# Mamba steps of 16 channels by 8 states: new step layout, a text position for every piece, and a reordered last layer

## The chip, the cores and the metric

The kernel runs on one core of one Trainium2 chip. The metric is the device time of one execution in microseconds (us); the number of record is the median over the runs of the kernel before. Engine names are those of the profile: PE (TensorE matmul), PEld (its weight loads), DVE (VectorE), ACT (ScalarE), POOL (GpSimd), SP (SyncE, which here issues DMAs).

## The reference

Four layers follow one another on an image of 2 x 64 x 96 x 96, all in float32. Cut to what matters:

```python
# layer 0: attention over all 9216 pixels of an image, then a 1x1 convolution with batch norm
x = bn(conv1x1(softmax(theta(x) @ phi(x)) @ g(x))) + x
# layer 1: depthwise and 1x1 convolution, batch norm, relu; layer norm; one Mamba over L = 9216
# layer 2: for the rows, then for the columns of the image: RMS norm, a forward and a backward
#          Mamba over L = 96, joined by a linear map, plus the input
# layer 3: a 3x3 filter per group of channels, its taps = tanh(W mean(x)), plus x

def mamba(h):                       # 128 inner channels d, 16 states s
    xm, z = split(h @ in_proj.T)
    xc = silu(causal_conv4(xm) + convd_b)
    dt, B, C = split(xc @ x_proj.T)             # 4, 16, 16 columns
    dt = softplus(dt @ dt_proj.T + dt_proj_b)
    A = -exp(A_log)                             # [d, s]
    # for each t:
    hc = hc * exp(dt[..., None] * A) + dt[..., None] * B[:, None, :] * xc[..., None]
    y  = einsum('bds,bs->bd', hc, C)
    return ((y + xc * Dp) * silu(z)) @ out_proj.T
```

## The kernel before

**Layer 0** (`layer0_direct`) is not touched. It fills the first 2400 us of the profiled execution.

**Layers 1 and 2** are a stream of 120 *units*, run by the class `Mamba`. A unit is one Mamba over a chunk of `CH` = 768 positions for one image of the batch: 24 units of layer 1, which carry their state from chunk to chunk (`u.carry`), and 96 units of layer 2, each with 8 whole sequences of 96 ("fresh"; the odd ones run backward). The 2048 recurrences of a unit (128 channels by 16 states) are laid on 128 partitions in 16 *steps*. A chunk has two halves of `HALF` = 384 positions; a half has 16 *turns* and a step takes two of them at once, 128 x 768 elements. In a turn, partition 8 s + i holds state s and channel 8 n + i (mod 128 over the turns), so 8 channels meet all 16 states and every turn rotates which channel a partition sees.

A step runs through these pieces:
- `read` (SP, L912): two DMAs bring dt and u = dt * xc, spread over the partitions, from a DRAM copy (`rows`, written twice one below the other by `step_write`, so that a turn is a plain window of 128 rows) into one of 6 `spread` buffers
- `decay` (ACT, L919): two Exp with a scale per partition, into an `h` buffer (9 of them)
- `inputs` (DVE, L929): u times B, into one of two PSUM places; B is spread to all partitions by the matmul of `shared` (L923), once for each half
- `scan` (DVE, L944, or L940 twice for a carried state): hc = decay * hc + input; then POOL multiplies by C (L945)
- `gather` (PE, L954): two matmuls of 128 x 128 sum over the states and put the channels in place in `y`; the first of a half adds xc * Dp (L951)

Around the steps stand the pieces of a unit: norm, convolution (L821/L827, read at L832), gate, silu (between two loads of ACT's table, L841 and L842), softplus (`step_read`, `step_exp`, `step_log` on ACT, then `step_kept`, `step_sum`, `step_dt` on POOL: L872, L875, L878), `step_u` (L882), `step_write`, C (`c_mm`, L898), and at the end `y_half` (L958), `y_read` (L961), `y_gate` (POOL, L964) and the `tail` projection (L987/L990). All but the steps' own share one PSUM tile of two banks (tag `m`).

**Order.** Tiles and semaphores are the framework's, but `run` issues everything in an order written out by hand, and each engine executes its instructions in the order of that text. `PIECES` gives each piece an offset in whole steps against its unit, alike for both layers; within a step the order is fixed (reads, decays, inputs, scan, gathers, pieces that read PSUM, the others). The first unit's head runs ahead alone, and one unit's worth of empty steps follows it. At two steps of every unit `next(other)` advances a generator that finishes the image of layer 1 and prepares the weights of the four Mambas of layer 2 (`mamba_weights`, L629 to L667, and `joined`) in the free space of `xa`.

**Layer 3** copies the image with mirrored borders into `upper` (DVE, L1250) and `lower`, computes the taps (L1255 to L1277), and filters: PE in four sets of rows with tiles of 32 x 32 (L1294, 16 matmuls for each tap, copied out by ACT at L1303) and DVE for the 28 rows at the top (L1313). It stands in a section of its own behind the Mamba stage.

Of the kernel before, what the change touches and what calls it, by code (L numbers as in the profile page):

```python
# [25 lines left out]
P = 128  # L26
# [9 lines left out]
NMAMBA = 5  # L36

# [34 lines left out]
def setup(ctx, tc, x, cols, mats, dtw):  # L72
# [42 lines left out]
    k.minus = const.tile([P, 1], FP, name="minus")  # L115
    nc.vector.memset(k.minus, -1.0)
# [91 lines left out]
def layer0_direct(k, scale, bias, pre):  # L208
# [9 lines left out]
    with (  # L218
# [19 lines left out]
        def product(lhsT, rhs, m, n):  # L238
            p = bank("m")[:m, :n]
            nc.tensor.matmul(p, lhsT=lhsT, rhs=rhs, start=True, stop=True)  # L240
            return p
# [321 lines left out]

class Carver:
# [16 lines left out]
def mamba_tables(k, pool):  # L581

    nc = k.nc
    G = P // 8
    t = SimpleNamespace()

    t.member = pool.tile([P, 8], FP, name="member")
    nc.vector.reduce_sum(t.member, k.ident.rearrange("p (g i) -> p i g", i=8), axis=AX.X)  # L590
    t.group = pool.tile([P, 2, G], FP, name="group")
    for j in range(2):
        nc.vector.reduce_sum(t.group[:, j], k.ident.rearrange("p (g i) -> p g i", i=8), axis=AX.X)

    pair = pool.tile([P, 2, P], FP, name="pair")
    nc.vector.tensor_copy(pair, k.ident.unsqueeze(1).to_broadcast([P, 2, P]))
    pair = pair.rearrange("p j c -> p (j c)")
    t.gather = [pair[:, P - 8 * n : 2 * P - 8 * n] for n in range(G)]

    t.centre = pool.tile([P, 2, C], FP, name="centre")  # L600
    for j in range(2):
        nc.vector.tensor_add(t.centre[:, j], k.ident[:, :C], k.ident[:, C:])
        nc.vector.tensor_scalar_add(t.centre[:, j], t.centre[:, j], -1.0 / C)
    t.centre = t.centre.rearrange("p j c -> p (j c)")
    return t


def scratch(k, t, pool):


    G = P // 8
    t.turned = pool.tile([P, G, G], FP, name="turned")
    two = t.group.rearrange("p j g -> p (j g)")
    for n in range(G):
        k.nc.vector.tensor_copy(t.turned[:, n], two[:, G - n : 2 * G - n])
    t.placed = pool.tile([P, D_STATE, 8], FP, name="placed")
    t.rates = pool.tile([P, P // 8, P // 8], FP, name="turned_rates")


def mamba_weights(k, w, pool, product, tables, i):  # L620
# [4 lines left out]
    G = P // 8  # L625


# [3 lines left out]
    nc.vector.tensor_mul(  # L631
        tables.placed,
        tables.member.unsqueeze(1).to_broadcast([P, D_STATE, 8]),
        a.unsqueeze(2).to_broadcast([P, D_STATE, 8]),
    )
    p = product(tables.placed.rearrange("p s i -> p (s i)"), tables.group[:, 0], P, G)
    yield
    nc.vector.tensor_mul(tables.rates, tables.turned, p.unsqueeze(1).to_broadcast([P, G, G]))
    w.rates = pool.tile([P, G], FP, name=f"rates{i}")
    nc.vector.reduce_sum(w.rates, tables.rates, axis=AX.X)  # L640
# [23 lines left out]
    bc = pool.tile([P, 2, D_STATE, 8], FP, name=f"bc{i}")  # L664
    for j in range(2):
        at = DT_RANK + j * D_STATE
        nc.vector.tensor_copy(bc[:, j], x_w[:, at : at + D_STATE].unsqueeze(2).to_broadcast([P, D_STATE, 8]))  # L667
    w.gate_w = in_w[:, P:]
    w.bc = [bc[:, j].rearrange("p s i -> p (s i)") for j in range(2)]
# [5 lines left out]
class Mamba:  # L675
# [15 lines left out]
    STEPS = P // 8  # L691
    READ = 5
    DECAY = 3
# [15 lines left out]
    def product(self, lhsT, rhs, m, n):  # L709
        p = self.ps_m.tile([P, 2 * NB], FP, tag="m", name="mm")[:m, :n]  # L710
        self.nc.tensor.matmul(p, lhsT=lhsT, rhs=rhs, start=True, stop=True)
        return p
# [44 lines left out]
    def norm_square(self, u):  # L757

        if u.carry:
            u.norm.x = self.work("xn", D_CONV - 1 + CH)  # L760
            u.sq = self.work("sq", bufs=1)
# [15 lines left out]
    def image_1(self, u):  # L777
        self.image_copy(u, 1)
        if u.norm.unit is u and not u.carry:
            u.sq = self.work("sq", bufs=1)  # L780
# [69 lines left out]
    def step_read(self, u):  # L850
# [5 lines left out]
        u.kept = self.by_half(self.work("kept", bufs=1))  # L856
# [4 lines left out]
    def step_exp(self, u):  # L861
        nc = self.nc
        nc.scalar.activation(u.e, u.e, AF.Exp, scale=-1.0)
        nc.scalar.activation(u.kept, u.e, AF.Identity, bias=1.0)
        nc.scalar.activation(u.kept, u.kept, AF.Identity, bias=self.k.minus)  # L865
# [5 lines left out]
    def step_kept(self, u):  # L871
        self.nc.gpsimd.tensor_sub(u.kept, u.e, u.kept)  # L872

    def step_sum(self, u):
        self.nc.gpsimd.tensor_add(u.log, u.log, u.kept)  # L875

    def step_dt(self, u):
        self.nc.gpsimd.tensor_add(u.dt, u.dt, u.log)  # L878
# [9 lines left out]
    def step_write(self, u):  # L888
        u.rows = self.dram.tile([2 * P, 2 * CH], FP, tag="rows", name="rows")
        for j in range(2):  # L890
            self.nc.sync.dma_start(out=u.rows[j * P : (j + 1) * P], in_=u.both)

    def c_mm(self, u):
        u.p = self.mm([(u.w.bc[1], self.halves(u.xc))])

    def c_read(self, u):
        u.C = self.work("C")
        self.nc.scalar.copy(u.C, u.p)  # L898
# [4 lines left out]
    def turns(step):  # L903
        half, m = divmod(step, Mamba.STEPS // 2)
        return half, (2 * m, 2 * m + 1)

    def read(self, u, step):
        half, turns = self.turns(step)
        u.dtu[step] = self.work("spread", 2 * CH, bufs=6)
        for q, n in enumerate(turns):  # L910
            row = u.rows[8 * n : 8 * n + P, bass.ts(half, CH)]
            self.nc.sync.dma_start(out=u.dtu[step][:, bass.ts(q, CH)], in_=row)  # L912

    def decay(self, u, step):

        h = u.h[step] = self.work("h", bufs=9)
        for q, n in enumerate(self.turns(step)[1]):
            dt = u.dtu[step][:, q * CH : q * CH + HALF]
            self.nc.scalar.activation(h[:, bass.ts(q, HALF)], dt, AF.Exp, scale=u.w.rates[:, n : n + 1])  # L919

    def shared(self, u, half):

        self.nc.tensor.matmul(self.B, lhsT=u.w.bc[0], rhs=u.xc[:, bass.ts(half, HALF)], start=True, stop=True)  # L923

    def inputs(self, u, step):

        bx = self.places[step % 2][1].rearrange("p (q t) -> p q t", q=2)
        x = u.dtu[step].rearrange("p (q a t) -> p q a t", q=2, a=2)[:, :, 1]
        self.nc.vector.tensor_mul(bx, x, self.B.unsqueeze(1).to_broadcast([P, 2, HALF]))  # L929

    def scan(self, u, step):
        nc = self.nc
        half, turns = self.turns(step)
        h, bx = u.h[step], self.places[step % 2][1]
        h2 = h.rearrange("p (q t) -> p q t", q=2)
        if u.carry:
            state = u.carry[:, turns[0] : turns[1] + 1]
            for q in range(2):
                at = bass.ts(q, HALF)
                nc.vector.tensor_tensor_scan(h[:, at], h[:, at], bx[:, at], state[:, q : q + 1], ALU.mult, ALU.add)  # L940
            nc.gpsimd.tensor_copy(state.unsqueeze(2), h2[:, :, HALF - 1 :])
        else:
            way = slice(None, None, -1) if u.rev else slice(None)
            nc.vector.tensor_tensor_scan(h[:, way], h[:, way], bx[:, way], 0.0, ALU.mult, ALU.add)  # L944
        nc.gpsimd.tensor_mul(h2, h2, u.C[:, bass.ts(half, HALF)].unsqueeze(1).to_broadcast([P, 2, HALF]))  # L945

    def gather(self, u, step):

        half, turns = self.turns(step)
        if turns[0] == 0:  # L950
            self.nc.tensor.matmul(self.y, lhsT=u.w.direct, rhs=u.xc[:, bass.ts(half, HALF)], start=True, stop=False)  # L951
        for q, n in enumerate(turns):
            rhs, stop = u.h[step][:, bass.ts(q, HALF)], n == self.STEPS - 1
# [467 lines left out]
```

## Time and profile before

| | us |
|---|---|
| runs shown | 7492.55, 7496.15, 7505.91; median 7496.15 |
| profiled execution, own time | 7498.15 |
| its span, first to last instruction | 7496.4 |
| first product of a Mamba step starts (L929) | 2449.9 |
| last scan ends | 7428.8 |
| last set of PE in layer 3 ends | 7491.5 |

The mean granted TensorE clock is 0.972 of full speed. Times of single instructions come from the profiled execution. A line of a group reads: source line, engine, operation, output and inputs with shapes, count, then busy time and mean duration, then the engine's idle time just before those instructions and what ended most of it. Since consecutive instructions of an engine overlap a little in the records, the pitch between two starts is shorter than a mean duration.

### The profile page before, as it was taken

To read this page: it belongs to the slowest core of one execution; us is meant where nothing else is said; L and a number is where in the kernel's file an instruction comes from. 1 tells how busy PE (TensorE), PEld (TensorE's weight loads), DVE (VectorE), ACT (ScalarE), POOL (GpSimd) and SP (SyncE) were. 2 spreads that over 40 slices of the span, in tenths; PEclk is the share of its full clock that TensorE was granted. 3 is DMA by queue.
4 is the path that set the end of the run, shared out by engine and by line. 5 is a ranking of instruction groups with operands and counts; after the bars stand their busy time and mean duration, and the time that the engine had idled before them with its cause. 6 is when DMAs were issued, how large, how long until landed. Compare 5 with 4: busy or idle time off the path is not lost.

```text
span 7496.4 us, 106738 instructions
## 1 busy us (share of the span) xinstructions
PE 6776.0 (90%) x35828; PEld 3025.7 (40%) x35828; DVE 6881.7 (92%) x5965; ACT 5307.7 (71%) x7425; POOL 4857.1 (65%) x3219
## 2 busy tenths in 40 slices
PE   9999999999998888888888888888898888888887
PEld 3333333333332344443444444444444444444443
DVE  6778787888886799999999999999999999999998
ACT  5555555555555777777877788888788787787884
POOL 0000000000000799998989999999999999999995
PEclk9999999999998899999999999999999999999998
DMA  1000000000000799998999999999999999999996
GB/s 46 1 1 1 1 1 1 3 5 6 6 6 29 279 322 326 327 326 302 352 330 342 345 354 351 351 350 349 355 350 353 353 351 354 352 351 350 354 353 227
DMA packets 595263, 1727.63 MB, mean 230 GB/s; under 512 B 66312, under 2 KB 68620, under 8 KB 594320
## 3 DMA queue, kind: packets, MB, share of 16 engines
q1 hardware_dynamic: 594264, 1719.41, 63.1%
q8 instruction: 283, 4.64, 0.2%
q14 instruction: 276, 2.26, 0.1%
q10 hardware_dynamic: 440, 1.32, 0.1%
HBM read 1522.68 MB, written 197.79 MB: 230 GB/s over the span
## 4 chain that ended last, share of the span: by engine, by line
PE 12%; DMA 10%; issue 10%; ACT 8%; POOL 8%; DVE 4%; SPq 1%; DVEq 0%; ACTq 0%; POOLq 0%
DMA spread<-rows 8%; PE y L954 7%; POOL h L945 5%; ACT h L919 4%; DMA rows<-dtu 3%; DVE place L929 2%; DVE h L944 2%; PE mm L725 2%; PE conv L827 1%; POOL dtu L878 1%; PE y L951 1%; POOL dtu L882 1%; PE B L923 1%; ACT L841 0%; ACT L842 0%
## 5 line engine op out<-in xcount | busy, mean ns | idle before, releaser
L945 POOL TENSOR_TENSOR h<-h,C 128x768 f32<-128x768 f32 x1920 | 3456.1, 1821 | 229.7 <-DVE h L944 197.1
L954 PE MATMUL y<-h,pair 128*128 128x384 f32 x7680 | 2807.9, 507 | 170.3 <-POOL h L945 168.9
L944 DVE TENSOR_TENSOR_SCAN h<-h,place 128x768 f32<-128x768 f32 x1536 | 2602.2, 1735 | 0.0
L919 ACT ACTIVATE h<-spread,xa 128x384 f32<-128x384 f32 x3072 | 1755.8, 608 | 506.9 <-DMA spread<-rows 473.8
L954 PEld LDWEIGHTS y<-h,pair 128*128 128x128 f32 x7680 | 1475.1, 197 | 1396.2 <-POOL h L945 420.3
L312 ACT ACTIVATE e<-f_exp 128x1024 f32<-128x1024 f32 x1296 | 1258.0, 1022 | 989.2 <-PE f_exp L298 989.2
L929 DVE TENSOR_TENSOR place<-spread,B 128x768 f32<-128x768 f32 x1920 | 1726.8, 944 | 98.5 <-PE B L923 49.9
L323 PE MATMUL y<-e,xb 64*64 64x512 f32 x10368 | 1233.3, 591 | 0.0
L298 PE MATMUL f_exp<-theta,phi 64*64 64x512 f32 x10368 | 1230.5, 589 | 2.0 <-DVE xb L283 1.4
L401 DVE TENSOR_TENSOR acc_e<-acc_e,e 128x1024 f32<-128x1024 f32 x612 | 771.3, 1260 | 302.4 <-ACT e L312 285.1
L337 POOL TENSOR_TENSOR ys<-ys,y_one 128x512 f32<-128x512 f32 x36 | 45.9, 1276 | 1457.4 <-DVE ys L336 1457.4
L410 DVE TENSOR_TENSOR acc_e<-acc_e,e 128x1024 f32<-128x1024 f32 x612 | 811.0, 1325 | 65.3 <-DVE acc_e L401 1.8
L940 DVE TENSOR_TENSOR_SCAN h<-h,state,place 128x384 f32<-128x384 f32 x768 | 713.3, 986 | 3.7 <-ACT h L919 3.6
L323 PEld LDWEIGHTS y<-e,xb 64*64 64x64 f32 x10368 | 394.1, 133 | 729.1 <-issue 723.7
L298 PEld LDWEIGHTS f_exp<-theta,phi 64*64 64x64 f32 x10368 | 395.5, 133 | 715.2 <-issue 703.2
L362 POOL TENSOR_TENSOR xa<-xa,t_att 64x512 f32<-64x512 f32 x36 | 54.3, 1510 | 756.8 <-ACT t_att L360 736.1
L919 ACT ACTIVATE h<-spread,rates 128x384 f32<-128x384 f32 x768 | 435.3, 608 | 104.2 <-DMA spread<-rows 93.5
L951 PE MATMUL y<-raw,xa 128*128 128x384 f32 x384 | 207.1, 626 | 222.3 <-ACT yg L961 194.3
L827 PE MATMUL conv<-xn,xa 64*128 64x384 f32 (+3 forms) x1536 | 271.9, 492 | 13.9 <-DVE xa L1161 4.1
L725 PE MATMUL mm<-raw,xa 128*128 128x384 f32 x768 | 279.5, 487 | 0.4 <-ACT dtu L859 0.3
L872 POOL TENSOR_TENSOR kept<-dtu,kept 128x768 f32<-128x768 f32 x120 | 218.8, 1823 | 66.0 <-ACT kept L865 64.1
L923 PE MATMUL B<-raw,xa 128*128 128x384 f32 x384 | 172.3, 531 | 73.5 <-DVE place L929 73.3
(226 smaller groups left out, 5526.0 us busy)
## 6 DMA issues: line engine op xcount, KB each, us to landing
spread<-rows SPq DMA_DIRECT2D x3840, 384.0 KB, 5.6
rows<-dtu SPq DMA_DIRECT2D x240, 768.0 KB, 5.1
image<-pre SPq DMA_DIRECT2D x11, 384.0 KB, 2.3
xb<-image SPq DMA_DIRECT2D x11, 384.0 KB, 6.8
xa<-in_x SPq DMA_DIRECT2D x1, 2304.0 KB, 22.7
xa<-in_x SPq DMA_DIRECT2D x3, 384.0 KB, 11.8
xb<-in_x SPq DMA_DIRECT2D x3, 384.0 KB, 12.7
xa<-in_x SPq DMA_DIRECT2D x1, 1152.0 KB, 18.2
```

Of the source, the lines that this page charges most:

```text
L298: nc.tensor.matmul(f[rows_of(half), bass.ts(side, NB)], lhsT=phi[at, m * P + half * C : m * P + (half + 1) * C], rhs=theta[at, bass.ts(i, ...
L312: nc.scalar.activation(e, f, AF.Exp)
L323: nc.tensor.matmul(ys[half][rows_of(side)], lhsT=g[at, m, :], rhs=e[at, bass.ts(side, NB)], start=m < 2, stop=m >= KEYS - 2,)
L401: nc.vector.tensor_add(block.acc, block.acc, es[0])
L410: nc.vector.tensor_add(block.acc, block.acc, es[1])
L725: self.nc.tensor.matmul(o, lhsT=lhsT, rhs=x, start=n == 0, stop=n == len(terms) - 1)
L919: self.nc.scalar.activation(h[:, bass.ts(q, HALF)], dt, AF.Exp, scale=u.w.rates[:, n : n + 1])
L929: self.nc.vector.tensor_mul(bx, x, self.B.unsqueeze(1).to_broadcast([P, 2, HALF]))
L940: nc.vector.tensor_tensor_scan(h[:, at], h[:, at], bx[:, at], state[:, q : q + 1], ALU.mult, ALU.add)
L944: nc.vector.tensor_tensor_scan(h[:, way], h[:, way], bx[:, way], 0.0, ALU.mult, ALU.add)
L945: nc.gpsimd.tensor_mul(h2, h2, u.C[:, bass.ts(half, HALF)].unsqueeze(1).to_broadcast([P, 2, HALF]))
L954: self.nc.tensor.matmul(self.y, lhsT=self.t.gather[n], rhs=rhs, start=False, stop=stop)
```

## The change

- **Layout of a step.** A step's 128 partitions now hold 16 channels (`SPAN`) by 8 states (`GROUP`); the 16 states are two parts (`PARTS`), the 128 channels eight blocks (`BLOCKS`). A step takes two blocks of one part in one half. Channels are not rotated: block b is the 16 channels from 32 (b mod 4) + 16 (b div 4). One `spread` serves the two steps (parts) with the same blocks, so a unit has 8 reads of two DMAs in place of 16; each source row is repeated over 8 partitions by the access pattern, and `rows` is written once.
- **B and C** are held per part: `shared` runs every 4 steps in place of every 8, `c_mm` once for each half (two matmuls each).
- **Gather** uses weights of 32 columns: a block goes to one of four column tiles, and the gathers of two steps are issued together.
- **Asides.** In the steps of `ASIDES` (5 for carrying units, 3 and 10 for fresh ones) the product `inputs` runs on POOL into an SBUF tile `bx`, from an SBUF copy of B (`b_copy`, ACT), and the decay goes to the PSUM place.
- **Softplus.** Four matmuls with the identity for each half (`sum_mm`) and a copy by ACT take the place of POOL's three additions.
- **Order.** Two tables, `CARRY` and `FRESH`, give every piece, the steps' own included, a fractional position. `next(other)` is called twice in the units that own a norm (each carrying unit, the first of each fresh pair).
- **Buffers.** `h` 8 for 9, `yg` 2 for 3; `sq` and the copy of B lie in `xa`.
- **Layer 3** stands in the same hand-ordered section. `Padded.early`, behind the last unit's `y_gate`, loads the Tanh table and makes the upper image in three copies; the last four rows are done with tiles of 64 x 64, and DVE has 32 rows.

```diff
 class Mamba:
-    STEPS = P // 8
-    READ = 5
-    DECAY = 3
+    STEPS = 16
+    HELD = 8
+    BX = 1
+    SPREADS = 6
+    YG = 2
...
-    def step_kept(self, u):
-        self.nc.gpsimd.tensor_sub(u.kept, u.e, u.kept)
-    def step_sum(self, u):
-        self.nc.gpsimd.tensor_add(u.log, u.log, u.kept)
-    def step_dt(self, u):
-        self.nc.gpsimd.tensor_add(u.dt, u.dt, u.log)
+    def sum_mm(self, u, half):
+        terms = (u.e, u.kept, u.log, u.dt)
+        self.half(u.sums, half, [(self.k.ident, lambda j, t=t: t[:, j]) for t in terms])
+    def sum_read(self, u):
+        self.nc.scalar.copy(u.dt, self.by_half(u.p))
...
-    def read(self, u, step):
-        u.dtu[step] = self.work("spread", 2 * CH, bufs=6)
-        for q, n in enumerate(turns):
-            row = u.rows[8 * n : 8 * n + P, bass.ts(half, CH)]
-            self.nc.sync.dma_start(out=u.dtu[step][:, bass.ts(q, CH)], in_=row)
+    def read(self, u, half, m):
+        d = u.dtu[half, m] = self.work("spread", 2 * CH, bufs=self.SPREADS)
+        for q in range(2):
+            rows = u.rows[channels(2 * m + q), bass.ts(half, CH)]
+            self.nc.sync.dma_start(
+                out=d[:, bass.ts(q, CH)], in_=rows.unsqueeze(1).to_broadcast([SPAN, GROUP, CH])
+            )
+    def room(self, u, step):
+        u.h[step] = self.by_half(self.work("h", bufs=self.HELD))
+        u.decay[step], u.bx[step] = u.h[step], self.place(step)
+        if step in self.aside(u):
+            u.decay[step], u.bx[step] = self.place(step), self.by_half(self.work("bx", bufs=self.BX))
...
-    def inputs(self, u, step):
-        bx = self.places[step % 2][1].rearrange("p (q t) -> p q t", q=2)
-        x = u.dtu[step].rearrange("p (q a t) -> p q a t", q=2, a=2)[:, :, 1]
-        self.nc.vector.tensor_mul(bx, x, self.B.unsqueeze(1).to_broadcast([P, 2, HALF]))
+    def b_copy(self, u):
+        u.B = self.Bs
+        self.nc.scalar.copy(u.B, self.B)
+    def inputs(self, u, step, engine):
+        B = (self.B if engine is self.nc.vector else u.B).unsqueeze(1).to_broadcast([P, 2, HALF])
+        engine.tensor_mul(u.bx[step], self.spread(u, step, 1), B)
...
-            self.nc.tensor.matmul(self.y, lhsT=self.t.gather[n], rhs=rhs, start=False, stop=stop)
+            y = self.y[bass.ts(block % 4, TILE)]
+            self.nc.tensor.matmul(y, lhsT=self.t.gather[block // 4], rhs=u.h[step][:, q], start=False, stop=stop)
...
-    PIECES = (
-        (-56, "image_0"),
...
+    CARRY = dict(
...
+    FRESH = dict(
+        norm_centre=-47.0,
...
+        conv=-27.35,
+        conv_read=-26.4,
+        gate_mm=-26.25,
+        gate_read=-25.85,
+        silu=-25.8,
+        step_mm=-25.05,
+        step_read=-24.5,
+        step_exp=-22.6,
+        step_log=-21.4,
+        sum_mm_0=-21.28,
+        sum_mm_1=-21.16,
+        sum_read=-19.5,
+        step_u=-13.25,
+        step_write=-9.35,
...
+        decay=-3.2,
+        aside_decay=-1.15,
+        aside=-2.65,
+        inputs=0.3,
+        scan=0.7,
+        gather=2.95,
+        shared=-1.55,
+        read_0=-8.2,
+        read_1=-8.15,
+        read_2=-5.7,
+        read_3=-0.55,
+        b_copy_0=-1.2,
+        b_copy_1=6.55,
+    )
+    ASIDES = ((5,), (3, 10))
...
+        for s in range(self.STEPS):
+            add(s + table["decay"], "room", s)
+            if s in asides:
+                add(s + table["aside_decay"], "decay", s)
+                add(s + table["aside"], "inputs", s, self.nc.gpsimd)
+            else:
+                add(s + table["decay"] + 0.01, "decay", s)
+                add(s - s % 2 + table["inputs"], "inputs", s, self.nc.vector)
+            add(s + table["scan"], "scan", s)
+            if s % 2:
+                add(s + table["gather"], "gather", s - 1)
+                add(s + table["gather"] + 0.001, "gather", s)
+            if s % 4 == 0:
+                add(s + table["shared"], "shared", *divmod(s // 4, PARTS))
...
 def layer3(k, padded, out):
-    SETS = (5, 5, 5, 2)
-    LOW = H - QUAD * sum(SETS)
+    SETS = ((4, 5), (4, 5), (4, 5), (2, 2))
+    LOW = H - sum(regions * n for regions, n in SETS)
```

## The prediction

> **What bounds the kernel now.** I read the page first, then the windows by stage, the waits of VectorE, and the timeline of a few steps. The page's first part names two nearly full engines; its costliest groups show whose work that is:
>
> ```profile
> PE 6776.0 (90%) x35828; PEld 3025.7 (40%) x35828; DVE 6881.7 (92%) x5965; ACT 5307.7 (71%) x7425; POOL 4857.1 (65%) x3219
> ...
> L945 POOL TENSOR_TENSOR h<-h,C 128x768 f32<-128x768 f32 x1920 | 3456.1, 1821 | 229.7 <-DVE h L944 197.1
> L954 PE MATMUL y<-h,pair 128*128 128x384 f32 x7680 | 2807.9, 507 | 170.3 <-POOL h L945 168.9
> L944 DVE TENSOR_TENSOR_SCAN h<-h,place 128x768 f32<-128x768 f32 x1536 | 2602.2, 1735 | 0.0
> ...
> L929 DVE TENSOR_TENSOR place<-spread,B 128x768 f32<-128x768 f32 x1920 | 1726.8, 944 | 98.5 <-PE B L923 49.9
> ```
>
> [...] The windows view (columns: length, then busy us of PE, PEld, DVE, ACT, POOL, clock, DMA share, GB/s) for most of layer 2:
>
> ```profile
> 3700.00:7200.00 3500.00, 3057.26 (x9347) 1535.47 (x9346) 3488.05 (x2791) 2811.50 (x4257) 3303.89 (x1945) 0.97 0.96 350
> ```
>
> VectorE is busy 3488 of 3500 us. POOL at 94%, DMA at 96%, PE at 87% and ACT at 80% all have some room. The waits view of that stretch confirms that the others wait, and VectorE does not:
>
> ```profile
> ACT h L919 <- DMA spread<-rows: 408.9, 714, 4.2
> ...
> PEld y L951 <- ACT yg L961: 234.3, 87, 5.9
> ...
> DVE place L929 <- PE B L923: 10.8, 13, 1.6
> ```
>
> ACT loses 409 us to late DMAs, yet the scan never sees it. So **VectorE's work sets the time of the stage**, and its price is the pitch between starts, not the mean:
>
> ```profile
> 7102.64 1.80 DVE L929 TENSOR_TENSOR place<-spread,B 128x768 f32<-128x768 f32 x2
> 7104.35 3.39 DVE L944 TENSOR_TENSOR_SCAN h<-h,place 128x768 f32<-128x768 f32 x2
> 7107.65 1.80 DVE L929 TENSOR_TENSOR place<-spread,B 128x768 f32<-128x768 f32 x2
> ```
>
> Two multiplications take 1.71 us (0.855 each), two scans 3.30, a fresh unit 8 x 5.01 = 40.1 us.
>
> [...] No gather of before is tiled, but layer 3 is (32 by 32):
>
> ```profile
> 5008.97 2.74 PE L954 MATMUL y<-h,pair 128*128 128x384 f32 x8
> ...
> 7452.73 29.90 PE L1294 MATMUL pc<-xa,diag 32*32 32x480 f32 x876 [3.08 <-DVE diag L1277]
> ```
>
> A matmul leaves two records. Untiled, one costs 2.74/4 = 0.685 us. Tiled, 876 records in 29.90 us, 32 records for each round of 16 tiles, give 1.09 us a round; a lone one of 480 columns would be 0.685 x 480/384 = 0.86. Overlap holds, at 1.27 times one matmul. [...]
> [...] L631, two SBUF inputs, takes 0.291 us with POOL idle and a median of 1.836 us beside it.
> [...] Here 1821 against 944 ns, 1.93 times.
>
> **The change, part by part.**
> 1. *Asides.* In two of 16 steps of a fresh unit (3 and 10) and one of a carrying unit (5) L929's multiplication goes to POOL. VectorE loses 96 x 2 + 24 x 1 = 216 of them: 216 x 0.855 = **-184.7 us**, on the path. The scan of an aside has its decay in PSUM and its input in SBUF, still one of each, so I price it as now; bounds -0.1 to +0.1 us each, +-22 in all.
> 2. *POOL.* Busy 3303.9 us for 86 units is 38.4 per unit. It loses three additions (L872, L875, L878) and gains two asides: -1 x 1.8, so 36.6 of the new unit's 40.1 - 1.7 = 38.4 us. A carrying unit loses three and gains one. Covered, narrowly, at 95%. An aside stands in POOL's order ahead of products with C; a scan waits for it only in its own step.
> 3. *PE.* Gathers become 32 columns wide, and two steps are issued together: four matmuls on four different column tiles, estimated 0.685 x 1.27 = 0.87 us. Eight such groups: 7.0 us in place of 21.9. Added per unit: eight matmuls of the sum of four terms (identity as weights), two of C, two of B; with direct 2, B 2, C 2, step 2 these are 20 x 0.685 = 13.7. Convolution 2.8, gate 0.9, mean 0.5, tail 2.9 stay. Sum 27.8 of 38.4 us: covered. [...]
> 4. *ACT.* 2811.5/86 = 32.7 per unit. Added: one read of the sums (0.78, as L898), a second read of C (0.78), two copies of B (0.45 each, as L961): 35.2 of 38.4, 92%. Covered if it does not idle; its waits for spreads (409 us in that window) should shrink.
> 5. *DMA.* Each spread now serves two steps: 1920 reads of 384 KB for 3840, 120 writes for 240. The queue at 96% falls to about half. Worth nothing by itself, since VectorE did not wait for it; SP's order keeps the write ahead of the reads of its unit. Whether a row read eight times over is slower isn't in the trace; bounds 0 to double, and at double the queue is where it was.
> 6. *Weights.* VectorE's part grows: a second product like L631 (4 x 1.84), two more copies like L667 per layer (8 x 0.62), less L638 and L640 (4 x 0.81): **+10 us** on the path with the small copies. `next(other)` moves to the first unit of each pair, twice each; VectorE executes the same calls, and 36 for the second half of layer 2 fit into 48 units.
> 7. *B.* One bank, now loaded every 4 steps rather than 8, in the 3.3 us of two scans; 0.7 of PE. Before it PE has gathers, which wait for POOL. VectorE lost 49.9 us to B, 30.3 of it once behind the first unit. Bounds -20 to +60; I take **+8**.
> 8. *Head and first gap.* Eight sums on a cold PE (up to 1.3 us each by the first head's rows: 2.9 us for two) and a read, for three POOL additions of 1.8: **+3** (0 to +7) before the first scan. The 30 us gap behind the first unit keeps its 16 empty steps: fewer POOL operations, but B now stands behind the next unit's sums. 0, bounds -15 to +10.
> 9. *End.* POOL now makes the borders, waiting for VectorE's copy, before the last gate:
>
> ```profile
> 7437.61 0.63 POOL L1248 COPY xa<-xa 128x88 f32<-128x88 f32 x2 [6.79 <-DVE xa L1250]
> 7438.19 1.80 POOL L964 TENSOR_TENSOR yg<-yg,raw 128x768 f32<-128x768 f32 x1
> 7440.05 0.29 PEld L725 LDWEIGHTS mm<-yg,xa 128*64 128x64 f32 x2 [7.50 <-POOL yg L964]
> 7449.73 1.28 ACT L1261 ACT_TABLE_LOAD   x1 [1.43 <-PE pf L1259]
> ```
>
> With the gate first it can start when L961 ends, 7432.95: -5.2. The Tanh table is loaded early: -1.3 [...]. The last set, 9.3 us with 288 records, becomes 72 in 64 by 64: estimated 9 x 0.34 x 1.27 = 3.9, -5.4 on PE; VectorE's rows grow from 28 to 32, 29.6 to 33.8 us, and become the last (PE 29.4 + 3.9 = 33.3). Together **-12** (-6 to -16).
>
> Sum: -184.7 + 10 + 8 + 3 - 12 = -175.7. Against the profiled execution's own 7498.15 us (its span 7496.4 and 1.75 around it) that is 7322.4, and the median of the runs, 7496.15, lies 2 below. I say **7322**.
>
> **The rivals.**
> *Column tiles don't overlap* (slower). All four read all 128 partitions, unlike layer 3's, and four streams per row group are what layer 3 does show. If they ran one by one, PE would need 20.8 + 21.9 = 42.7 us per unit against VectorE's 38.4: 120 x 42.7 = 5124 us for a stage of 4979 now, less 40 of head and gaps, about 7680. It decides where a group of four exceeds (38.4 - 20.8)/8 = 2.2 us. Chance 0.05.
> *New waits.* ACT at 92% and POOL at 95% run in one fixed order each, and every piece shares one PSUM tile, with 1 to 2 us round trips between PE and ACT; the decay of an aside must also wait until the scan two steps earlier has freed its PSUM place, and blocks ACT's queue meanwhile. The trace shows ACT waiting 114 us for the convolution in 86 units. At 1 us of stalls in VectorE per unit: +120, 7440; at 1.46 the gain is gone. Against it: decays run some 3 steps ahead of the scan, 7 us. Chance 0.25: 0.18 still faster, 0.03 even, 0.04 slower.
> *The moved product costs VectorE anyway*: [...] it would lose up to 1.8 us each, 216 x 1.8 = 389 for 185 saved, 7710. The scans of now (one SBUF, one PSUM input, 1715 to 1754 ns beside a busy POOL) speak against it. I put it, with the unforeseen, within the slower 0.09 of the two above.
>
> **How the numbers follow.** Forecast 0.70, 7280 to 7365 by the bounds above. The new waits reach up from there; the range 7275 to 7415 leaves out their upper part, the first rival and a gap that vanishes wholly. Within 0.2% (15 us) a measurement cannot tell a change: 0.03; faster 0.88; slower 0.09.
>
> **What would show it.** VectorE busy near 99% of the stage with 1704 products on VectorE and 216 on POOL; scans still at 1.735 us; gathers of four within about 1 us; DMA share near 0.5; waits of ACT for spreads mostly gone; a fresh unit every 38.4 us; the gate ahead of the borders. I am wrong if units take over 39.5 us: then the waits of VectorE name whether ACT's decays, PE's B or POOL's asides are late.

## The result, and the profile after

The median of the changed kernel is 7478.9 us, against 7500.8 us for the kernel before on the same chip (six runs each): a ratio of 0.9975, with a 95% interval of 0.9964 to 0.9985. The change gains 22 us where 176 were forecast, and 7479 lies outside the range of 7275 to 7415. The profiled execution has a span of 7479.7 us and a mean TensorE clock of 0.941.

The page of the kernel after, its first part and the groups that answer to those shown of before:

```profile
PE 6309.8 (84%) x38502; PEld 2338.3 (31%) x38502; DVE 6739.8 (90%) x5732; ACT 5470.8 (73%) x7876; POOL 4609.8 (62%) x3074
...
L1002 POOL TENSOR_TENSOR h<-h,C 128x768 f32<-128x768 f32 x1920 | 3454.6, 1818 | 364.8 <-DVE h L1000 308.5
L1000 DVE TENSOR_TENSOR_SCAN h<-h,place 128x768 f32<-128x768 f32 x1344 | 2288.2, 1736 | 12.6
...
L986 DVE TENSOR_TENSOR place<-spread,B 128x768 f32<-128x768 f32 x1704 | 1548.2, 948 | 214.4 <-ACT xa L982 78.9
...
L1013 PE MATMUL y<-h,held 128*32 128x384 f32 x7680 | 1041.1, 532 | 212.3 <-POOL h L1002 212.3
...
L986 POOL TENSOR_TENSOR bx<-spread,xa 128x768 f32<-128x768 f32 x216 | 392.3, 1816 | 14.0 <-ACT xa L982 13.2
```

The 216 products are on POOL (the last line); VectorE keeps 1704. Its scans last 1736 ns as before, and the gathers cost PE 1041 us where they cost 2808. What is new stands at the end of the line of VectorE's products (L986 on DVE): 214.4 us of idle time ahead of them, where L929 had 98.5.

The windows view of the same stretch of layer 2:

```profile
3700.00:7200.00 3500.00, 2709.07 (x11546) 1037.89 (x11546) 3398.52 (x2649) 2965.29 (x4643) 3180.94 (x1875) 0.93 0.68 177
```

VectorE was busy 3488 of these 3500 us and is now busy 3398.5. By the starts of the scans, the stretch holds 87.2 units where it held 86.4. From the first scan of the first fresh unit (at 3571.9 us) to the first scan of the last (7384.4) lie 95 units, so a fresh unit takes 40.13 us; before (3537.2 to 7390.3) it took 40.56. The forecast was 38.4, and over 39.5 was its sign of being wrong. Per unit of the stretch VectorE works 39.0 us and idles 1.2. The carrying units, counted in the same way, became longer: 44.9 us after 44.0. No engine is full.

The waits view of VectorE, from 2400 us to the end, tells whom it waits for (total us, times, longest us), first before and then after:

```profile
DVE place L929 <- PE B L923: 49.9, 17, 30.3
DVE place L929 <- DMA spread<-rows: 48.4, 2, 47.4
...
DVE place L986 <- ACT xa L982: 78.9, 95, 2.6
DVE place L986 <- PE B L978: 72.6, 32, 38.8
DVE place L986 <- DMA spread<-rows: 58.6, 3, 52.8
```

After the change, the third line is mostly the first unit's head, before the stage (52.8 us of it; 47.4 before). The first is `b_copy`, ACT's copy of B for the asides, of which the kernel before has none. The second is the matmul that loads B; 38.8 of it is the gap behind the first unit, 30.3 before. The timeline of PE, ACT and VectorE shows how the copy for step 10 comes late, ahead of step 8 (start, length, and in brackets the wait):

```profile
5007.11 0.85 PE L1013 MATMUL y<-h,held 128*32 128x384 f32 x8
...
5008.68 0.91 PE L978 MATMUL B<-raw,xa 128*128 128x384 f32 x2 [0.72 <-DVE place L986]
5009.34 1.48 ACT L859 ACTIVATE raw<-raw 128x1536 f32<-128x1536 f32 x1
5010.84 1.28 ACT L860 ACT_TABLE_LOAD   x1
...
5012.13 0.48 ACT L982 COPY xa<-B 128x384 f32<-128x384 f32 x1
...
5012.64 1.83 DVE L986 TENSOR_TENSOR place<-spread,B 128x768 f32<-128x768 f32 x2 [0.72 <-ACT xa L982]
```

B is ready at 5009.6. ACT is in the silu and in the table load behind it, and copies B only at 5012.13. VectorE doesn't need the copy, yet its products start when the copy ends. The trace shows the order, not the reason for it: ACT's copy comes first in the text, and VectorE's product, which reads the same `B`, waits 0.72 us for ACT. Ahead of step 8 (50 of the 87 us of such delay in the table below) the copy stands behind ACT's table load, as here; ahead of step 0 (36 us) it stands behind a decay.

To add up all such delays I took the starts of VectorE's instructions in the stage and summed what exceeds the usual pitch of each kind of pair by more than 0.04 us. Before it is 57 us, after it is 215:

| VectorE is late ahead of | before | after | ended by |
|---|---|---|---|
| fresh steps 0 and 8 | 12 | 87 | ACT's copy of B (before: PE's B) |
| carrying step 12, fresh step 12 | 0 | 36 | PE's B |
| the first gap | 30 | 39 | PE's B |
| the scan of step 2, whose product stands alone | 0 | 20 | its own product |
| the lone product of step 11 | 0 | 11 | the place that scan 9 holds |
| the aside scan of step 10 | 0 | 8 | PE, ACT |
| the rest | 14 | 13 | |

The same starts close the account of the stage. The 216 products at their pitch of 0.849 us are -183.4 us, the delays +157.7, pitches that grew by less than 0.04 us each +6.5, and VectorE's other pieces (the weights of layer 2, 40.9 us before and 49.6 after) +8.7. That makes -10.5, and the stage (first product to last scan) went from 4978.9 to 4968.4.

At the end the gate now stands ahead of the borders, as the timeline of POOL shows:

```profile
7427.29 2.47 POOL L1023 TENSOR_TENSOR yg<-yg,raw 128x768 f32<-128x768 f32 x1 [2.18 <-ACT yg L1020]
7429.70 0.26 POOL L1381 COPY xa<-xa 128x96 f32<-128x96 f32 x1
```

From the last scan to the end of the span it takes 58.1 us, 9.5 less than before.

### The profile page after: what moved, and what is told of

Its sections match the earlier page's. It is cut to its first block, busy times and chain, and to the rows that moved or that the text cites. A ratio compares the mean times of both kernels' runs of the same rounds, so it can differ in the third digit from the quotient of the medians.

```text
span 7479.7 us, 106202 instructions
## 1 busy us (share of the span) xinstructions
PE 6309.8 (84%) x38502; PEld 2338.3 (31%) x38502; DVE 6739.8 (90%) x5732; ACT 5470.8 (73%) x7876; POOL 4609.8 (62%) x3074
## 3 DMA queue, kind: packets, MB, share of 16 engines
q1 hardware_dynamic: 300184, 869.94, 44.9%
q14 instruction: 229, 1.88, 0.1%
## 5 line engine op out<-in xcount | busy, mean ns | idle before, releaser
L1000 DVE TENSOR_TENSOR_SCAN h<-h,place 128x768 f32<-128x768 f32 x1344 | 2288.2, 1736 | 12.6
L986 DVE TENSOR_TENSOR place<-spread,B 128x768 f32<-128x768 f32 x1704 | 1548.2, 948 | 214.4 <-ACT xa L982 78.9
L973 ACT ACTIVATE h<-spread,xa 128x384 f32<-128x384 f32 x2688 | 1459.9, 607 | 80.9 <-PE y L1013 56.1
L1013 PE MATMUL y<-h,held 128*32 128x384 f32 x7680 | 1041.1, 532 | 212.3 <-POOL h L1002 212.3
L978 PE MATMUL B<-raw,xa 128*128 128x384 f32 x960 | 497.6, 604 | 323.1 <-DVE place L986 310.4
L920 PE MATMUL mm<-raw,xa 128*128 128x384 f32 x960 | 386.4, 527 | 138.4 <-ACT C L924 78.2
L1013 PEld LDWEIGHTS y<-h,held 128*32 128x32 f32 x7680 | 198.7, 111 | 933.9 <-POOL h L1002 516.7
L743 PE MATMUL mm<-dtu,ident 128*128 128x384 f32 x960 | 418.2, 541 | 9.6 <-ACT xb L1048 4.9
L973 ACT ACTIVATE h<-spread,rates 128x384 f32<-128x384 f32 x720 | 394.9, 605 | 31.1 <-PE y L1013 16.8
L986 POOL TENSOR_TENSOR bx<-spread,xa 128x768 f32<-128x768 f32 x216 | 392.3, 1816 | 14.0 <-ACT xa L982 13.2
L973 ACT ACTIVATE place<-spread,xa 128x384 f32<-128x384 f32 x384 | 224.0, 583 | 199.8 <-DVE h L1000 193.3
```

The costliest lines, as they stand in the source:

```text
L973: self.nc.scalar.activation(u.decay[step][:, q], dt[:, q], AF.Exp, scale=rate)
L978: self.nc.tensor.matmul(self.B, lhsT=u.w.bc[0][part], rhs=x, start=True, stop=True)
L986: engine.tensor_mul(u.bx[step], self.spread(u, step, 1), B)
L1000: nc.vector.tensor_tensor_scan(*flat, 0.0, ALU.mult, ALU.add)
L1013: self.nc.tensor.matmul(y, lhsT=self.t.gather[block // 4], rhs=u.h[step][:, q], start=False, stop=stop)
```

## The experiments

Ratios are to the kernel before, timed on the same chip, with 95% intervals; kernels are compared with each other by their medians. "Delays" are VectorE's, summed as above.

**1. The asides out, and the copies out.** e1 leaves all 216 products on VectorE, so that only the new layout and order are left. e2 keeps the asides, but they multiply by zeros, and ACT copies nothing.

```diff
 e1, e2:
-        b_copy_0=2.7,               # CARRY
-        b_copy_0=-1.2,              # FRESH
-        b_copy_1=6.55,
 e1:
-    ASIDES = ((5,), (3, 10))
+    ASIDES = ((), ())
 e2:
-        B = (self.B if engine is self.nc.vector else u.B)...
+        B = (self.B if engine is self.nc.vector else self.Bs)...   # Bs set to 0 once
```

> The new layout, order and last layer without any aside: all 1920 products on VectorE and no copies of B. Theory (local waits: the changed kernel lost what the asides saved to two things, VectorE's products waiting for ACT's copy of B, 88 us, and a lone product in front of its scan, 31 us): VectorE gets back 216 x 0.85 = 184 us of products and sheds 88 + 31 + 8 us, so 7479 + 57 = about 7536 us, with no wait of products for ACT. Rival (general load: ACT and POOL near their limits in a fixed order stall VectorE whatever it is that waits): the 130 us of waits stay, 7479 + 150 = about 7630 us.

> The changed kernel with its asides, but without ACT's copies of B: the asides read a tile of zeros, so B is left out of one or two steps of 16 and the values are not the reference's. Local waits: 86 us of waits in front of steps 0 and 8 go, and a few us behind them: about 7390 us. General load: ACT loses 0.9 us of 35 per unit, the waits move to the next late piece, 7450 to 7479 us.

e1: 7573.2 us, 1.0100 (1.0083 to 1.0117), between the two theories. The layout and order alone, with the new last layer, cost 75 us, and the asides gain 94 of the 183 that their products weigh. e1's delays are 135 us, 78 above before, about those 75; 83 of them stand ahead of step 12, nearly all ended by PE's B. e2: 7418.9, 0.9890 (0.9874 to 0.9907), again between the two: the copies cost 60 us. Of the 87 us ahead of steps 0 and 8, 6 are left, but 19 came up ahead of step 12 (55 after 36) and 8 ahead of the aside's scan of step 10. So the copies are one cause; the second, B at step 12, remains in both.

**2. The copies moved.** e3 lets ACT copy B later, behind VectorE's products of the same pair of steps, and POOL's aside product follows the copy; the fresh units alone are touched.

```diff
-        b_copy_0=-1.2,
-        b_copy_1=6.55,
+        b_copy_0=0.35,
+        b_copy_1=8.35,
...
-                add(s + table["aside"], "inputs", s, self.nc.gpsimd)
+                at_pool = table["aside"] if u.carry else {3: -2.6, 10: -1.6}[s]
+                add(s + at_pool, "inputs", s, self.nc.gpsimd)
```

> All the work of the changed kernel; only the text order of fresh units differs: ACT's copy of B stands behind VectorE's products of the same step pair instead of before them, and POOL's aside right after it. Local waits: VectorE no longer waits for the copy, ACT waits for VectorE instead; 75 to 86 us go, about 7400 us, unless POOL's asides then come late for their scans. General load: asides or decays become late instead, less than 25 us go, 7455 us or more.

7433.5 us, 0.9908 (0.9892 to 0.9925). Nothing is computed otherwise, and 45 us come from the text position of two copies and of the asides behind them, less than the 75 to 86 of the theory. The waits of VectorE no longer list ACT's copy among the large ones; the largest is PE's B:

```profile
DVE place L986 <- PE B L978: 101.9, 59, 38.2
DVE place L986 <- DMA spread<-rows: 57.6, 3, 52.7
```

**3. The lone product.** e4 puts the scan of step 3, an aside, between the product of step 2 and its scan, so that no scan follows the product that it reads.

```diff
-            add(s + table["scan"], "scan", s)
+            first = not u.carry and s == 3
+            add(s + table["scan"] - 1.05 * first, "scan", s)
```

> The changed kernel, but in step pair 2, 3 of fresh units the scan of the aside (3) is issued before the scan of step 2, so that the pair's lone product on VectorE is not followed at once by the scan that reads it. Local waits: 96 x 0.21 = 20 us go, 7459 us. Rival (the pause is no matter of dependence but a price of any lone product): no change, 7479 us.

7541.4 us, 1.0051 (1.0035 to 1.0068): a miss. The 20 us of the lone product went, but 18 came up ahead of the product of step 4, which now stands right behind the scan that holds its place. The aside's scan starts 53 us late in all; the likely reason is its decay, which ACT can write only into the PSUM place that scan 1 frees, though the profile names it for only 10 of the 53.

**4. B ahead of the tail.** The B of step 12 is issued behind the tail of the unit before and the sums of the next. e5 moves both behind it, e6 joins this with e3, and e7 is e6 with the asides at steps 2 and 10.

```diff
 CARRY: tail_0, tail_1, tail_read = 25.55, 25.6, 26.05 -> 26.3, 26.35, 26.8
 FRESH: tail_0, tail_1, tail_read = 23.7, 24.6, 25.8 -> 26.5, 26.6, 27.0
        sum_mm_0, sum_mm_1 = -21.28, -21.16 -> -20.8, -20.7
 e7:
-    ASIDES = ((5,), (3, 10))
+    ASIDES = ((5,), (2, 10))
```

> The changed kernel with one edit of PE's text order: the tail projection, its read and the two sum pieces stand behind the load of B for step 12 instead of before it. Theory (B is late at step 12 because PE's queue stands at the tail, which waits until ACT's softplus read has freed the shared PSUM tile): the waits of products for PE's B at step 12, 26 us in carrying and 10 us in fresh units, go; 7443 us, if the waits for ACT's copies stay as they are. Rival (PE itself is late there, whatever stands in front): B is no earlier, 7470 to 7480 us.

> e3_copy_late and e5_b_first together. If the two waits are separate: from e3's 7434 us another 31 + 21 us (its waits for B at step 12) go, about 7385 us. If one wait only gives way to the next piece that is late: 7420 to 7435 us.

> e6_both with the fresh asides in steps 2 and 10 in place of 3 and 10, so that in both pairs the scan of the aside, which needs no product of VectorE, directly follows the lone product. Dependence: the lone product costs 0.12 us beyond its pitch in place of 0.21, 96 x 0.1 = 9 us less than e6_both, if POOL's aside and ACT's decay, now needed one scan earlier, are in time. If they are late (one scan of 1.66 us less room): 10 to 60 us more than e6_both.

e5: 7878.1 us, 1.0505 (1.0488 to 1.0523). e6: 7680.2, 1.0241 (1.0224 to 1.0258). e7: 7674.5, 1.0233 (1.0216 to 1.0250). e5 and e6 missed; e7's 6 us below e6 lie within the spread of its runs (7670.9 to 7703.7) and decide nothing. In e5 the delay ahead of step 12 is gone, and some 335 us stand ahead of the fresh step 0. The waits of VectorE and of ACT in e5:

```profile
DVE place L986 <- ACT xa L982: 407.4, 196, 8.3
```

```profile
ACT dtu L902 <- PE mm L743: 342.7, 98, 7.2
ACT xb L1051 <- PE mm L743: 209.6, 47, 6.4
```

The tail now stands in the way of the sums, ACT waits for both in its fixed order, and the copy of B and the decays are queued behind those waits. PE's B is late there as well: in e6, where the copy stands later, 229 us remain ahead of the fresh step 0, and PE's B ends them.

**5. DMA traffic, and the sums on POOL.** e8 adds one DRAM copy of 384 KB for each spread. e9 is e1 with the three additions of softplus back on POOL, spread over later positions, in place of the sums on PE.

```diff
 e8, behind the second DMA of read:
+            if q:
+                self.nc.sync.dma_start(out=self.dram.tile([P, CH], FP, ...), in_=u.rows[:, bass.ts(half, CH)])
 e9:
+    sum_mm_0: tensor_add(u.kept, u.e, u.kept)      # POOL
+    sum_mm_1: tensor_add(u.log, u.log, u.kept)
+    sum_read: tensor_add(u.dt, u.dt, u.log)
```

> The changed kernel with an idle DMA added for each spread (384 KB from the rows to a place in DRAM that nobody reads), so that the DMA share rises from 0.68 towards 1. If halving the DMA traffic was worth nothing, as VectorE waited for no transfer: 7470 to 7490 us, though ACT waits for spreads again. If the lower traffic was part of what the change gained: 20 us or more slower than the changed kernel's 7479 us.

> e1_no_asides with the softplus sum back on POOL: three additions in place of the eight identity matmuls and ACT's read; the layout of steps, B every four steps, C in two pieces and the tables of positions stay. Theory (the shared PSUM tile m and PE's fixed order are what make B late: m is held 30.6 us of each unit in e1 and 23.5 in the kernel before, and the sum is 7.5 of it): most of e1's 83 us of waits for B at step 12 go, 7573 - 60 to 83 = about 7490 to 7515 us, about the kernel before. Rival (loading B every four steps is the price, whatever stands in m): the waits stay, 7560 us or more.

e8: 7523.2 us, 1.0033 (1.0019 to 1.0047), 44 above the changed kernel. The DMA share rose from 0.68 to 0.83 and the landing of a spread from 6.1 to 6.7 us. The extra DMAs also stand in SP's queue, and this run doesn't separate the two. e9: 7591.0, 1.0123 (1.0106 to 1.0140). The shared PSUM tile was held 23.2 us per unit again, as before, where e1 holds it 30.6, but the waits for B stayed (delays of 58 at the fresh step 12, 31 at the carrying one, 23 at step 0). A shorter hold of that tile by the sums alone did not bring B in time. It isn't a clean exclusion, since with less work PE's mean clock fell from 0.932 to 0.891. But one wait of PE is the same in e1 and e9, in the stretch from 3700 to 7200 us:

```profile
PE mm L743 <- ACT dtu L876: 103.0, 42, 2.5
```

It is the first matmul of the tail (it reads `yg`), which needs the shared tile and waits until ACT has read the step's matmul out of it (`step_read`). In the text it stands shortly ahead of the B of step 12.

**6. Shorter and earlier pieces.** e10 is e3 with `log` as the last term of the sums in both halves, so that PE can start before ACT's Ln. e11 is e3 with the tail ahead of the step matmuls, e12 has both. e16, tried later, is e10 with the early tail in the carrying units alone.

```diff
 e10:
+        for j in range(2):                              # sum_mm_0
+            for n, t in enumerate((u.e, u.kept, u.dt)): matmul(u.sums[j], ident, t[:, j])
+        for j in range(2):                              # sum_mm_1
+            matmul(u.sums[j], ident, u.log[:, j])
 e11, e12: CARRY tail_0, tail_1, tail_read = 23.5, 23.55, 23.9; FRESH = 22.5, 22.55, 22.85
 e16: CARRY alone
```

> e3_copy_late with the terms of the softplus sum in another order: the three terms that are ready early for both halves, then the logarithm for both, so that two matmuls and not six stand behind the logarithm. Theory of the shared tile: it is held some 2.5 us less per unit (7.9 in e3), and the 16 us of waits for B in front of step 0 shrink; 7410 to 7425 us. Rival: the sum is not on the chain, 7434 us.

> e3_copy_late with the tail projection and its read moved in front of the step's matmul, into the 4 us in which ACT is at silu and the shared PSUM tile is free, in place of behind the softplus read. Theory of the shared tile: the tail no longer waits for the softplus read, so B for step 12 is in time without making the sum later (as e5 did); 21 + 31 us of waits go, about 7385 us. Rival (any place of the tail delays what follows): B or the decays become late elsewhere, 7430 us or more.

> e11_tail_early and e10_log_last together: if both work and are separate, about 7370 us; if the tail's place costs elsewhere, between the two of them or above e3's 7434 us.

> The best order so far, with the tail two steps earlier in the 24 carrying units alone. Theory: in the trace with all tails early the carrying units waited 17 us, against 38 with the tail where it was, and only the fresh units lost: 7425 - 21 = 7400-7410. Rival (the tail's wait moves to ACT's decays there as well): 7425 or more.

e10: 7425.1 us, 0.9900 (0.9883 to 0.9916), in the range of the theory, and the delay ahead of step 0 fell from 16 to 9 us; but the interval overlaps widely with e3's, so a gain this small is not shown by the times alone. e11: 7672.0, 1.0228 (1.0211 to 1.0245), and e12: 7657.5, 1.0208 (1.0191 to 1.0225), both misses: with a tail in it, ACT waits for the tail's matmuls, and the copy of B and the aside's decay are queued behind. The waits of VectorE in e11:

```profile
DVE place L986 <- ACT xa L982: 217.3, 50, 6.9
DVE h L1000 <- ACT place L973: 70.6, 69, 1.2
```

The loss was in the fresh units only, and e16 shows it: **7409.2 us, 0.9887 (0.9870 to 0.9903)**, 85 below before and the lowest median of all, though its interval overlaps with those of e2 and e10. The delays of the carrying units fell from 38 to 14 us, 25 of it ahead of step 12, and the forecast of 7400 to 7410 held.

**7. The reload itself.** e13, e14 and e15 leave out the second load of B in each half, from e1, e2 and e10.

```diff
-            if s % 4 == 0:
+            if s % 8 == 0:
                 add(s + table["shared"], "shared", *divmod(s // 4, PARTS))
```

> Kernel without asides and copies, and B loaded only at steps 0 and 8 as in the kernel before (steps 4 to 7 and 12 to 15 of each unit then multiply by the first eight states' B: that part of the computation is changed). Theory (the reload of B at steps 4 and 12, queued on PE behind the tail and its round trip with ACT, is what the new layout costs): VectorE's waits before step 12, 83 us without asides, go, and the time falls from 7573 to 7490-7505, that of the kernel before. Rival (the layout costs elsewhere: ACT fuller, the shared PSUM tile held longer): the wait moves to step 0 or to the decays, and the time stays above 7545.

> Asides as in the change, but they multiply by zeros (no copy of B by ACT), and B loaded only at steps 0 and 8 (both parts of the computation are changed). Theory: without the copies the time was 7419; the waits for B at step 12, 55 us there, go too: 7355-7370. What then stands between it and the forecast of 7322 is the lone product's dependence (some 31 us) and the longer first gap (8). Rival (other waits fill in): above 7395.

> The best order so far (copies late, log last in the sums) with B loaded only at steps 0 and 8 (steps 4 to 7 and 12 to 15 multiply by the first eight states' B). Theory: 7425 less the 49 us of waits before step 12: 7370-7385. Rival (the waits are those of the tail's round trip with ACT, whatever PE loads): 7410 or more.

e13: 7523.4 us, 1.0045 (1.0028 to 1.0061): 50 of the layout's 75 us go with the reload, and 30 stay, for 44 us of delay are now ahead of step 0. e14: 7430.2, 0.9916 (0.9899 to 0.9932), where e2 had 7418.9; e15: 7432.2, 0.9917 (0.9900 to 0.9933), where e10 had 7425.1. My theory fell: with the asides in, the reload's removal gains nothing. In e14 the 55 us ahead of step 12 became 54 ahead of step 0: PE comes late to the next load of B. In e15 the wait moved otherwise: 24 us ahead of the carrying step 0, and 25 ahead of the aside's scan of step 10, which waits mostly for its decay. What PE does before a late load in e14, by its timeline and by the windows view:

```profile
6233.62 1.65 PE L1008 MATMUL y<-raw,xa 128*128 128x384 f32 x2 [3.72 <-ACT yg L1020]
...
6250.51 1.49 PE L1013 MATMUL y<-h,held 128*32 128x384 f32 x4 [2.36 <-POOL h L1002]
6252.78 1.65 PE L743 MATMUL mm<-dtu,ident 128*128 128x384 f32 x2 [0.77 <-ACT dtu L882]
6254.53 1.65 PE L743 MATMUL mm<-kept,ident 128*128 128x384 f32 x2
...
6260.28 1.01 PE L743 MATMUL mm<-kept,ident 128*128 128x384 f32 x2
6261.13 0.81 PE L743 MATMUL mm<-log,ident 128*128 128x384 f32 x2
6261.77 0.81 PE L743 MATMUL mm<-dtu,ident 128*128 128x384 f32 x2
```

```profile
6235.00:6252.00 17.00, 11.78 (x59) 3.83 (x58) 16.97 (x14) 14.70 (x22) 16.94 (x11) 0.90 0.81 220
6252.00:6260.00 8.00, 7.03 (x12) 3.19 (x11) 8.00 (x7) 7.88 (x13) 6.41 (x5) 0.50 0.36 97
6260.00:6267.00 7.00, 7.00 (x34) 3.00 (x33) 6.19 (x6) 4.03 (x7) 4.63 (x4) 0.95 1.05 245
```

The granted clock (third number from the end) is 0.50 in the 8 us from 6252, and the matmuls of the sums start 1.75 us apart there; then it is 0.95, and the last ones start 0.64 apart. The pitch grew 2.7 times where the clock is 0.53 of the later one; the rest is left unexplained. What lowered the clock isn't shown either: the stretch from 6235 to 6252 us, behind PE's wait of 3.72 us, has a mean of 0.90, and PE's waits in it are 1.06, 0.63, 1.16 and 2.36 us. In e14 the fresh units fall into two kinds by turns: in one the sums take 9.7 us (median), and 37 of the 39 late starts of the fresh step 0 stand behind these; in the other they take 6.0. This suggested one more cause, the clock, which was lower in runs with less work for PE: in the stretch from 3700 to 7200 us it is 0.97 before, with PE busy 3057 us, 0.93 after, with 2709, and 0.92 in e14, with 2694.

**8. More work for PE.** e17 and e18 add to e14 and e16 six matmuls of zero weights per unit, ahead of gathers, which change no sum.

```diff
         if part == m == 0:
             ...
+        elif step % 2 == 0:
+            self.nc.tensor.matmul(self.y, lhsT=self.t.zero, rhs=u.xc[:, bass.ts(half, HALF)], start=False, stop=False)
```

> e14 (asides on zeros, B loaded at steps 0 and 8) with six more 128 by 128 matmuls per unit, of zero weights, each ahead of a gather of four: 120 x 6 x 0.65 = 468 us more work for PE. Theory ([...] its sums of four terms take 9.5 us where 5.2 would do, and B behind them is late): the mean clock rises from 0.927 to 0.95 or more, the sums shorten, VectorE's 54 us of waits at step 0 shrink by half or more, 7430 falls to 7385-7410. Rival (only the fixed order makes B late): six matmuls more delay it further, 7440 or more.

> e16 (the best order so far) with the same six zero matmuls per unit. Its clock is 0.948 already and its sums take 6.5 us. Theory: a small gain, 7390-7409. Rival (order only): PE's longer work delays B and the gathers, 7415 or more.

e17: 7453.6 us, 0.9939 (0.9925 to 0.9953), 23 above e14. e18: 7494.2, 0.9996 (0.9987 to 1.0004), 85 above e16. The mean clock rose from 0.927 to 0.959 and from 0.948 to 0.969; the time got longer all the same. In e17 the long sums shortened only from 9.7 to 8.9 us, and the delay of the fresh step 0 behind them fell from 28 to 11 us, but behind the other sums it rose from 3 to 22. In e18 the delay ahead of the fresh step 12 rose from 24 to 71 us. So the zero matmuls cost more than the clock gave back, by standing ahead of B in PE's order. Whether the slow clock is part of what makes B late isn't separated from their own work by these two runs. The windows view of e18 over the stretch of layer 2:

```profile
3700.00:7200.00 3500.00, 3018.19 (x12596) 1184.81 (x12595) 3395.27 (x2650) 2968.64 (x4642) 3179.51 (x1873) 0.98 0.69 177
```

PE is at 86% here, and more work per unit already costs time: by estimate 6 x 0.65 = 3.9 us more of PE (e14's last sums start 0.64 us apart), and measured 85/120 = 0.7 us more per unit.

## Why the prediction was wrong

VectorE's work was priced rightly; the failed step is the cover. The prediction took ACT and PE as covered from their busy shares: part 4 ("covered if it does not idle") put the copies of B at nothing, where they delay VectorE by 74 us more than before, and part 7 put B at +8, where step 12 alone took 36.

- *Parts 1 and 2, asides and POOL.* The moved products left VectorE (-183.4 us by the pitch), POOL works 3180.9/87.2 = 36.5 us per unit (36.6 forecast), and scans with swapped operands last 1740 ns, the others 1736. An aside's product takes POOL 1816 ns, where VectorE's take 948: 1.92 times, as the 1821 against 944 of before. What failed is a small term: I priced every aside at the pitch of a product. The scan of step 2, whose product stands alone right ahead of it, starts 0.21 us later than the pitch, and the lone product of step 11 waits 0.12 for its place: 31 us, outside my bound of +-22.
- *Part 3, PE.* The group of four gathers takes 0.85 us, 0.87 forecast. The column tiles overlap (0.85 us is the median of 960 groups; where the granted clock was 0.50, as at 5000.8 us, one took 1.51). PE works 31.1 us per unit, 27.8 forecast; in part its clock is lower (0.93 for 0.97). "Covered" was read from a share of 27.8 in 38.4. e17 and e18 show that this room can't be used at any place of this order: work ahead of a B load delays it.
- *Part 4, ACT.* 2965.3/87.2 = 34.0 us per unit, 35.2 forecast, so it had the time. Its waits for spreads went as forecast (2 us in the stretch, after 409), but it now waits 171.5 us there for the scan that frees the PSUM place of an aside's decay. I asked only whether it had time, not what stands behind its new read of B. A copy takes 0.48 us of ACT, and VectorE's products start late behind the copies by 87 us in all (60 us of time by e2, of which e3 got 45 back by position alone).
- *Part 5, DMA.* The share fell from 0.96 to 0.68, not to 0.5, though the traffic halved (350 to 177 GB/s): a byte takes the queue 1.4 times as long. That less traffic is worth nothing by itself is not shown, since e8's +44 us is not separated from SP's queue.
- *Part 6, weights.* +8.7 us for +10. Six of the eight products with two SBUF inputs that fall into the stage take 1.84 to 1.88 us, two 0.28.
- *Part 7, B.* +8, bounds -20 to +60. The 36 us of step 12 lie within that bound, but with the asides out (e1) it is 83 us of delay, and e13 puts 50 us of time on the reload. I had sized it by the waits of before alone, and left out the tail and the sums that now stand in front of the load. The tail's wait for ACT is shown above.
- *Parts 8 and 9.* The head came 3.3 us later (+3 forecast; the clock granted in the forecast's 2.9 us for two was 0.50, from 2408.9 to 2411.8 us of before), the first gap 8.5 longer (0), the end 9.5 shorter (12).

With the measured terms in their places the sum is -183.4 + 8.7 (weights) + 74.4 (steps 0 and 8, the copies) + 36.0 (step 12) + 31.4 (lone products) + 8.5 (gap) + 8.5 (aside of step 10) - 1.1 (the rest) + 6.5 (small pitches) + 3.3 (head) - 9.5 (end) = -16.7, and the spans differ by 7479.7 - 7496.4 = -16.7.

Of the rivals, *New waits* is what came, at 158/120 = 1.3 us per unit, and it had a chance of 0.25. It named the ring of PE and ACT through the shared tile, the order, and the decay of an aside; it didn't name the copy of B, which was the largest. "Column tiles don't overlap" and "the moved product costs VectorE anyway" are refuted by 0.85 us and 1740 ns.

What stays open: which link of the ring of PE, ACT and the shared tile limits it once the copies are moved, and what part the clock has in it. e3 and e16 gain by order (e10 by its trace), e5 to e7, e11 and e12 lose by it, and in e13 to e15 the wait moves on to other pieces, in e13 and e14 to the next load of B. No order tried comes near 7322; the best, e16, still has 145 us of delays.

## What to carry to other kernels

When work is moved from the bounding engine to others, list for every new read of a shared PSUM tile who else reads that tile, and where in the reader's queue it stands: here ACT had the 0.48 us for each copy, and VectorE was late behind the copies by 87 us in all. A busy share of 77 to 91% on the neighbours (PE 77, ACT 85, POOL 91 in the stretch of layer 2) was not room in this order written by hand; ask of each piece what is in front of it on its engine at the moment at which the bounding engine needs it. And try positions first: here two copies moved by less than two steps, with the asides behind them, gained 45 us, twice what the whole change gained.

## What the hardware showed unexpectedly

- Four column tiles of 128 by 32 that read all 128 partitions overlap: 0.85 us for four matmuls of 384 columns, untiled 2.74 (granted clock 1.00 at the group of 5007.1 us).
- A VectorE scan that reads the product just ahead of it starts 1.07 us after it. Where a scan follows a product that it doesn't read, the pitch is 0.86, and 0.87 behind the lone product of step 11.
- With less work for PE (2709 us for 3057) its mean clock over the layer 2 stretch fell from 0.97 to 0.93. In e14 it was 0.50 from 6252 to 6260 us, in the middle of a unit; PE's longest wait from 6237 to 6252 us was 2.36 us. With matmuls of zeros the mean of the stretch was 0.98 in e18, after 0.94 in e16, and the kernel was 85 us slower.
- The DMA queue was 0.68 busy at 177 GB/s, where before it was 0.96 busy at 350: the spreads that repeat each row over 8 partitions came with 1.4 times the queue time per byte. Whether the repeated rows are the cause is not shown.
